# One core, conv-scan-attention block: a norm's factor moved behind its matmul, paired attention tiles, a split last projection, and new planner windows

## The chip, the cores and the metric

The kernel runs on one core of a Trainium2 chip. The metric is the device time of one execution in microseconds, taken as the median of several runs. Five engines work side by side, each on its own queue in order: PE (matmuls), DVE (VectorE), ACT (ScalarE), POOL (GpSimd) and SP, which here issues every DMA.

## What is computed

Input x is 8 images of 384 channels and 32 x 32 pixels, so 1024 tokens each. Two layers follow each other.

```
layer 0   xn  = rmsnorm over channels (x)
          per direction (forward, backward): u, z = in_proj(xn); u = silu(conv1d4(u))
              dt, B, C = x_proj(u);  delta = softplus(dt_proj(dt))
              h_t = exp(delta * A) * h_(t-1) + delta * u * B      384 channels x 16 states, 1024 steps
              y = sum over states(h * C) + u * D;   out_proj(y * silu(z))
          x1  = x + res * (scale * (fwd + bwd) + sigmoid(dwconv3x3(xn)) * xn)
layer 1   x2  = x1 + Wo * causal attention(layernorm(x1)), 6 heads of 64
          out = x2 + kron(p1, p2) * gelu(kron(f1, f2) * layernorm(x2))      (384 -> 1536 -> 384)
```

A layernorm subtracts the mean over the 384 channels and divides each token by its deviation. The first matmul of the last block is linear in the channels and has no bias, so a factor per token can be applied in front of it or behind it.

## The kernel before

The tiles are channels on the 128 partitions (three tiles of 128 channels) by 1024 tokens; HALF is 512 tokens, one PSUM bank of float32.

*The scan* (`scans` and `group`). For every image there are 96 steps: six blocks of 64 channels, two directions, and eight groups of 8 channels x 16 states = 128 rows. A step loads delta broadcast to the states into a tile dA (a DMA, 512 KB, of 12 such slots), takes its exp on ACT (L1007), spreads delta * u over the states with two matmuls into a ring of three PSUM banks, multiplies the two banks by B on DVE (L1035), scans 1024 tokens on DVE (L1041), multiplies by C on POOL (L1045) and sums the states on PE into the bank y. The operand of the spread is a tile du, loaded from DRAM array dusd, where delta * u lies as three bf16 parts (`delta`: POOL subtracts what was cast, L926, ACT casts the next part, L918, a DMA writes it).

*Around the scan*, for each image b: `project` (rmsnorm and in_proj of u), `gates` (in_proj of z), `prepare` (conv1d, x_proj), `deltas` (softplus and the parts), `local` (the 3 x 3 convolution), `finish` (out_proj, L1076 adds into x1), `layernorm`, `attention`, `mix` (Wo), `forward` (the last block).

*Attention* (`attend`): for each pair of heads and each 128 queries, the keys up to the diagonal come in one or two segments of up to 512. Scores on PE, maximum on DVE (L1201), exp on ACT (L1208), division on POOL (L1254), transposes of 128 x 128 on PE into a PSUM bank (L1261), copy to SBUF on ACT (L1268), context on PE. Weights p and their transposes pT had one tile for each head, 1024 keys wide.

*The norm* (`layernorm`): the mean comes from a matmul with ones (pm), DVE subtracts it (L1096), ACT squares (L1106), a matmul with ones sums (pv), ACT takes ln and exp in place for 1/deviation, and DVE multiplies each of the six half tiles by it (L1120). `forward` then multiplies by kr1 (py), copies to y (L1352), and goes on with the wide layer (ph, gelu, pz) and the last matmul (pe).

*The order.* Nothing runs in the order of the source. Each operation is recorded with an estimated cost and a due time; `Plan.run` then does a list scheduling over the five queues and four shared PSUM banks, 26 general SBUF slots and the slots of the scan, and the result is written out as a fixed order per engine. Due times come from windows: `stretch(span, b)` spreads a stage's operations over span x PERIOD after HEAD + b x PERIOD. The due time decides which of several ready operations goes first; on the chip nothing waits for it. The images overlap: while image b is scanned, b + 1 is prepared (`deltas`), b + 2 projected, and layer 1 of b - 1 runs. From image 2 to image 5 the order repeats.

Two lines set what follows from a window:

```
o.at = self.t0 + (self.t1 - self.t0) * done / total - early
a = o.at - (self.STAY if e == "ACT" and o.table in (None, table) else 0.0)
```

Of the kernel before, what the change touches and what calls it, by code (L numbers as in the profile page):

```python
# [12 lines left out]
ALU = mybir.AluOpType  # L13
# [4 lines left out]
P = 128  # L18
# [265 lines left out]
def conv_attn_hybrid_kernel(  # L284
# [49 lines left out]
    def half(hf):  # L334
        return slice(hf * HALF, (hf + 1) * HALF)

    def chans(c):
        return slice(c * P, (c + 1) * P)
# [94 lines left out]
    def bank(name):  # L433
        return Val("psm", [P, HALF], name)
# [12 lines left out]

    EVICT, MOVE, SUMS, PRODUCTS, DECAY, LOAD, PARTS = 154.0, 6.5, 31.9, 10.24, -27.73, -210.33, -103.58  # L450

    PROJECT, GATES, CONV, DELTA = (-1.488, -1.378), (-1.161, -1.106), (-0.901, -0.877), (-0.865, -0.39)
    LOCAL, OUTPUT, NORM, ATTEND = (0.78, 0.902), (0.999, 1.029), (1.126, 1.206), (1.226, 1.771)
    MIX, FORWARD = (1.75, 1.765), (1.898, 1.935)

    PROJECT0, EARLY, CONV0, DELTA0 = (-166.005, -75.933), (-268.945, -79.299), (87.042, 114.273), (95.896, 180.005)
    GATES0, LATE, PROJECT1, GATES1 = (198.993, 214.377), (111.423, 394.173), (-14.138, 120.69), (257.236, 258.236)
    CONV1, DELTA1, LAYER1 = (241.746, 250.867), (238.85, 495.647), (502.538, 846.683)

    class Window:  # L460

# [586 lines left out]
    def finish(b, x1):  # L1048

        s = b % 2  # L1050
        yg = []
        wo = tl(f"wout_{b}", [P, CT, C])
        dma(lambda: wo.t, lambda: out_wT.rearrange("(c p) e -> p c e", p=P), [], [wo], P * CT * C * 4)
        for c in range(CT):
            t = tl(f"yg_{b}_{c}")
            for a in range(2):
                v = ygd[s][2 * c + a]
                dma(
                    lambda t=t, a=a: t.t[a * HC : (a + 1) * HC, :], lambda v=v: v.t.rearrange("(h p) t -> p h t", p=HC),
                    [v], [(t, a)], HC * L * 4,  # L1060
                )
            yg.append(t)
        for m in range(CT):
            for hf in range(NH):
                p = bank(f"pg_{b}_{m}_{hf}")

                accumulate(
                    [
                        (lambda p=p, m=m, hf=hf, c=c: (p.t, wo.t[:, c, chans(m)], yg[c].t[:, half(hf)]), [yg[c], wo])
                        for c in range(CT)  # L1070
                    ], p, pe(HALF), [x1[m]],
                )

                def add(p=p, m=m, hf=hf):
                    t = x1[m].t[:, half(hf)]
                    nc.vector.scalar_tensor_tensor(t, p.t, rsm.t, t, ALU.mult, ALU.add)  # L1076

                op("DVE", dve(HALF), add, [p, rsm], [(x1[m], hf)])
            dma(lambda m=m: x1d[s].t[chans(m)], lambda m=m: x1[m].t, [x1[m]], [(x1d[s], m)], P * L * 4)

    def layernorm(dst, src, n):

        for hf in range(NH):
            p = bank(f"pm_{n}_{hf}")

            accumulate(
                [(lambda p=p, hf=hf, c=c: (p.t, ones, src[c].t[:, half(hf)]), [(src[c], hf)]) for c in range(CT)],  # L1090
                p, pe(HALF), dst,
            )
            for c in range(CT):
                op(
                    "DVE", dve(HALF),
                    lambda p=p, hf=hf, c=c: nc.vector.scalar_tensor_tensor(  # L1096
                        dst[c].t[:, half(hf)], p.t, -1.0 / C, src[c].t[:, half(hf)], ALU.mult, ALU.add
                    ), [p, (src[c], hf)], [(dst[c], hf)],
                )
        for hf in range(NH):  # L1100
            sqs = [tl(f"lsq_{n}_{hf}_{i}") for i in range(2)]
            p = bank(f"pv_{n}_{hf}")
            for c in range(CT):
                op(
                    "ACT", act(HALF),
                    lambda hf=hf, c=c, sqs=sqs: nc.scalar.activation(  # L1106
                        sqs[c // 2].t[:, half(c % 2)], dst[c].t[:, half(hf)], AF.Square
                    ), [(dst[c], hf)], [(sqs[c // 2], c % 2)], holds=sqs,
                )
            accumulate(  # L1110
                [
                    (lambda p=p, c=c, sqs=sqs: (p.t, ones, sqs[c // 2].t[:, half(c % 2)]), [(sqs[c // 2], c % 2)])
                    for c in range(CT)
                ], p, pe(HALF),
            )
            op("ACT", 2 * act(HALF) + 0.1, lambda p=p: rsqrt_mean(p.t, eps5), [], [p], table=EXP)
            for c in range(CT):
                op(
                    "DVE", dve(HALF),
                    lambda p=p, hf=hf, c=c: nc.vector.tensor_mul(dst[c].t[:, half(hf)], p.t, dst[c].t[:, half(hf)]),  # L1120
                    [p], [(dst[c], hf)],
                )

    def attention(b, x1):
# [45 lines left out]
        def attend(hp, i):  # L1170
# [3 lines left out]
            top, bottom = slice(0, HD), slice(HD, P)  # L1174
            nk = (i + 1) * P
            segs = [(k0, min(nk, k0 + HALF)) for k0 in range(0, nk, HALF)]
            ps = [tl(f"p_{n}_{hh}") for hh in range(2)]

            mx = Val("sm", [P, 2, 2], f"mx_{n}")
            den = Val("sm", [P, 2, 2], f"den_{n}")  # L1180
            for g, (k0, k1) in enumerate(segs):
# [23 lines left out]
                for hh in range(2):  # L1205

                    def exps(sc=sc, g=g, k0=k0, k1=k1, hh=hh):
                        nc.scalar.activation(  # L1208
                            ps[hh].t[:, k0:k1], sc[hh].t[:, 0 : k1 - k0], AF.Exp, bias=mx.t[:, g, hh : hh + 1],
                            accum_out=den.t[:, g, hh : hh + 1],  # L1210
                        )

                    op(
                        "ACT", act(k1 - k0) + 0.25, exps, [(mx, (g, hh)), sc[hh]], [(ps[hh], g), (den, (g, hh))],
                        table=EXP,
                    )
            if len(segs) > 1:
# [27 lines left out]
                op("POOL", 0.35, scales, [fac], [den])  # L1245
            else:
                op("DVE", 0.16, lambda: nc.vector.reciprocal(den.t[:, 0, :], den.t[:, 0, :]), [], [den])
            pT = [tl(f"pT_{n}_{hh}", [P, L // P, P]) for hh in range(2)]
            for g, (k0, k1) in enumerate(segs):
                for hh in range(2):  # L1250

                    def norm(g=g, hh=hh, k0=k0, k1=k1):
                        t = ps[hh].t[:, k0:k1]
                        nc.gpsimd.tensor_scalar(t, t, den.t[:, g, hh : hh + 1], 1.0, ALU.mult, ALU.mult)  # L1254

                    op("POOL", 0.15 + (k1 - k0) * 1.06e-3, norm, [den], [(ps[hh], g)])
                    t = bank(f"t_{n}_{g}_{hh}")

                    def turn(t=t, hh=hh, k0=k0, k1=k1):
                        for j in range(k0 // P, k1 // P):  # L1260
                            nc.tensor.transpose(  # L1261
                                t.t[:, j * P - k0 : (j + 1) * P - k0], ps[hh].t[:, j * P : (j + 1) * P], ident
                            )

                    op("PE", 0.05 + 0.12 * (k1 - k0) / P, turn, [(ps[hh], g)], [t], holds=pT)

                    def keep(t=t, hh=hh, k0=k0, k1=k1):
                        nc.scalar.copy(  # L1268
                            pT[hh].t[:, k0 // P : k1 // P, :].rearrange("p j t -> p (j t)"), t.t[:, 0 : k1 - k0]
                        )  # L1270

                    op("ACT", act(k1 - k0), keep, [t], [(pT[hh], g)])
            pc = bank(f"pc_{n}")

            cT = cTs[hp]
            for j0 in range(0, i + 1, 4):

                def context(js=range(j0, min(j0 + 4, i + 1))):
                    for j in js:
                        for hh, rows in enumerate((top, bottom)):  # L1280
                            mm(
                                pc.t[rows, 0:P], v.t[:, j * P + hh * HD : j * P + (hh + 1) * HD], pT[hh].t[:, j, :],
                                j == 0, j == i,
                            )

                op(
                    "PE", 0.05 + 0.24 * min(4, i + 1 - j0), context, [(t, j0 // 4) for t in pT] + [(v, j0 // 4)], [pc],
                    holds=[cT],
                )

# [44 lines left out]
    def forward(b, x2):  # L1335

        xn2 = [tl(f"xn2_{b}_{m}") for m in range(CT)]
        layernorm(xn2, x2, f"f{b}")
        y, z = tl(f"fy_{b}"), tl(f"fz_{b}")
        for hf in range(NH):  # L1340
            p = bank(f"py_{b}_{hf}")
# [8 lines left out]
                ], p, pe(HALF), [y],  # L1350
            )
            op("ACT", act(HALF), lambda p=p, hf=hf: nc.scalar.copy(y.t[:, half(hf)], p.t), [p], [(y, hf)])  # L1352
        for hf in range(NH):
            pz = bank(f"pz_{b}_{hf}")
            for a in range(FT // RG):
# [43 lines left out]

    PERIOD, HEAD = 417.04, 72.53

    def stretch(span, b):
        return Window(span[0] * PERIOD, span[1] * PERIOD, HEAD + b * PERIOD)
# [19 lines left out]
    for b in range(B):  # L1425
# [13 lines left out]
        with stretch(OUTPUT, b):  # L1439
            finish(b, x1)  # L1440
        with stretch(NORM, b):
            layernorm(x1, x1, f"a{b}")
        with stretch(ATTEND, b):
            cTs = attention(b, x1)
        with stretch(MIX, b):
# [79 lines left out]
```

## Time and profile before

| what | us |
|---|---|
| median of 3 runs | 4113.69 (4110.54 to 4115.77) |
| the profiled execution | 4114.34 |
| its span, first to last instruction | 4112.4 |
| first scan starts / last scan starts | 164.1 / 3837.8 |
| busy: PE, DVE, ACT, POOL | 3511.7, 3430.8, 2815.4, 3000.8 |
| mean granted clock of PE | 0.926 |
| DMA | 859 MB, mean 209 GB/s |

A row of the groups reads: line, engine, operation, output <- inputs, shapes, count, then busy microseconds and mean nanoseconds of one, then idle time of the engine just before these and what ended it. A row of the stretches gives the stretch, its length, and for each engine the busy time and the number of instructions, then the granted PE clock, the DMA share and GB/s. A row of the waits reads: who waited for whom, the total, how often, the longest. A row in order of time begins with start and duration; SPq is the DMA queue. Each float32 matmul of the program leaves two records.

### The profile page before, as it was taken

Reading aid. Unit: us, or ns where it says so; the run is one execution under the profiler, and the core shown is the slowest. Engines: PE = TensorE matmul, PEld = TensorE weight load, DVE = VectorE, ACT = ScalarE, POOL = GpSimd, SP = SyncE. Lnnn points to the kernel's source line nnn. Section 1 sums busy time; section 2 is a strip of 40 time slices with the busy share of each in tenths; the row PEclk is TensorE's granted clock in tenths of the full one; section 3 lists DMA queues with packets and bytes.
Section 4 is the critical chain, followed back from the end, with each engine's and each line's share of the span. In section 5 each row is a group of like instructions: output and inputs, shape, how many; then the busy total and the mean of one; then the engine's idle time right before and its main releaser. Section 6 shows DMA issues by size and latency. Waiting matters only on the chain. (4 is left out here: it accounts for less than half of the span.)

```text
span 4112.4 us, 54637 instructions
## 1 busy us (share of the span) xinstructions
PE 3511.7 (85%) x17970; PEld 1407.7 (34%) x17970; DVE 3430.8 (83%) x3661; ACT 2815.4 (68%) x4547; POOL 3000.8 (73%) x2370
## 2 busy tenths in 40 slices
PE   6466658899998999898998899988999888898898
PEld 2111112443234422443234432444234432443363
DVE  2399989989989899888989899889998899999522
ACT  3766447775787758885778857786787766665364
POOL 1889786997589955997579965998479965775231
PEclk9687679899999999899999999999998899999999
DMA  7899897579976898669976798669975697559100
GB/s 243 233 258 275 254 263 203 156 227 256 265 207 181 233 265 242 189 207 240 271 211 196 218 260 248 197 199 246 253 230 174 177 255 203 141 161 228 48 9 35
DMA packets 302003, 858.96 MB, mean 209 GB/s; under 512 B 38312, under 2 KB 91576, under 8 KB 301720
## 3 DMA queue, kind: packets, MB, share of 16 engines
q1 hardware_dynamic: 301720, 855.47, 74.6%
q8 instruction: 143, 2.34, 0.2%
q14 instruction: 140, 1.15, 0.1%
HBM read 696.44 MB, written 160.68 MB: 208 GB/s over the span
## 5 line engine op out<-in xcount | busy, mean ns | idle before, releaser
L1045 POOL TENSOR_TENSOR dA<-dA,bc 128x1024 f32<-128x1024 f32 x768 | 1810.6, 2365 | 724.5 <-DVE dA L1041 638.7
L1041 DVE TENSOR_TENSOR_SCAN dA<-dA,ring 128x1024 f32<-128x1024 f32 x768 | 1755.5, 2286 | 91.4 <-ACT dA L1007 27.6
L1035 DVE TENSOR_TENSOR ring<-ring,bc 128x512 f32<-128x512 f32 x1536 | 1071.2, 697 | 286.1 <-PE ring L327 171.8
L1007 ACT ACTIVATE dA<-dA,nA 128x1024 f32<-128x1024 f32 x768 | 860.8, 1145 | 249.8 <-DMA dA<-ded 245.1
L327 PE MATMUL ring<-du,dup 32*128 32x512 bf16 x1536 | 318.6, 410 | 384.4 <-DVE dA L1041 339.0
L327 PE MATMUL y<-dA,sel 128*32 128x512 f32 x3072 | 533.5, 659 | 28.6 <-POOL dA L1045 26.2
L1208 ACT ACTIVATE p<-s,mx 128x512 f32<-128x512 f32 (+3 forms) x576 | 330.9, 581 | 99.7 <-DVE mx L1201 98.8
L1201 DVE TENSOR_REDUCE mx<-s 128x1 f32<-128x512 f32 (+3 forms) x576 | 286.0, 546 | 134.1 <-PE s L327 130.4
L1254 POOL TENSOR_SCALAR p<-p,den 128x512 f32<-128x512 f32 (+3 forms) x576 | 329.1, 590 | 79.0 <-issue 47.0
L327 PEld LDWEIGHTS <-dup 32*128 32x128 bf16 x1536 | 73.1, 92 | 887.1 <-DVE dA L1041 779.9
L1268 ACT COPY pT<-t 128x512 f32<-128x512 f32 (+3 forms) x576 | 258.1, 483 | 163.1 <-PE t L1261 156.2
L1261 PE MATMUL t<-ident,p 128*128 128x128 f32 x1728 | 298.1, 304 | 74.3 <-ACT pT L1268 26.2
L327 PE MATMUL s<-k,q 64*128 64x512 f32 (+3 forms) x1152 | 301.8, 571 | 20.6 <-ACT p L1208 19.1
L327 PE MATMUL pi<-xp,win 128*128 128x512 f32 x576 | 287.7, 621 | 3.5 <-DMA win<-in_in_wT 2.0
L1261 PEld LDWEIGHTS t<-ident,p 128*128 128x128 f32 x1728 | 206.1, 152 | 212.1 <-POOL p L1254 83.7
L1461 ACT ACT_TABLE_LOAD x210 | 269.4, 1283 | 4.5 <-PEq L1514 0.8
L327 PE MATMUL pc<-pT,v 128*64 128x128 f32 x3456 | 261.9, 294 | 10.1 <-ACT pT L1268 5.6
L327 PEld LDWEIGHTS pc<-pT,v 128*64 128x64 f32 x3456 | 204.4, 146 | 105.6 <-ACT pT L1268 38.6
L918 ACT CAST part<-u 128x1024 bf16<-128x1024 f32 x144 | 150.3, 1044 | 88.7 <-POOL u L926 49.1
L926 POOL TENSOR_TENSOR u<-u,part 128x1024 f32<-128x1024 f32 x96 | 205.0, 2135 | 5.6 <-ACT part L918 5.5
L327 PEld LDWEIGHTS y<-dA,sel 128*32 128x32 f32 x3072 | 82.3, 113 | 287.2 <-issue 137.9
L327 PEld LDWEIGHTS s<-k,q 64*128 64x128 f32 x1152 | 116.7, 197 | 144.4 <-ACT p L1208 64.4
(183 smaller groups left out, 4714.5 us busy)
## 6 DMA issues: line engine op xcount, KB each, us to landing
dA<-ded SPq DMA_DIRECT2D x768, 512.0 KB
ct<-urd SPq DMA_DIRECT2D x96, 513.5 KB
du<-dusd SPq DMA_DIRECT2D x96, 512.0 KB
xs<-xpd SPq DMA_DIRECT2D x96, 432.8 KB
dusd<-part SPq DMA_DIRECT2D x288, 128.0 KB
ded<-de SPq DMA_DIRECT2D x48, 512.0 KB
uz<-uzd SPq DMA_DIRECT2D x48, 512.0 KB
bc<-bcd SPq DMA_DIRECT2D x32, 512.0 KB
```

The costliest lines, as they stand in the source:

```text
L327: return nc.tensor.matmul(out_, lhsT=lhsT, rhs=rhs, start=first, stop=last)
L926: "POOL", pool(L), lambda part=part: nc.gpsimd.tensor_sub(du.t, du.t, part.t), [part], [du]
L1007: "ACT", act(L) + 0.1, lambda: nc.scalar.activation(dA.t, dA.t, AF.Exp, scale=nA.t[:, g : g + 1]),
L1035: uses("DVE", nc.vector.tensor_mul(to, to, bc.t[:, 0, half(hf)]), [bank_of(v)])
L1041: i = nc.vector.tensor_tensor_scan(dA.t[:, rev], dA.t[:, rev], t[:, rev], 0.0, ALU.mult, ALU.add)
L1045: op("POOL", pool(L), lambda: nc.gpsimd.tensor_mul(dA.t, dA.t, bc.t[:, 1]), [(bc, 1)], [dA], at=at - PRODUCTS)
L1201: lambda sc=sc, g=g, w=k1 - k0, hh=hh: nc.vector.tensor_reduce(mx.t[:, g, hh : hh + 1], sc[hh].t[:, 0:w], AX.X, ALU.max, negate=True), [sc ...
L1208: nc.scalar.activation(ps[hh].t[:, k0:k1], sc[hh].t[:, 0 : k1 - k0], AF.Exp, bias=mx.t[:, g, hh : hh + 1], accum_out=den.t[:, g, hh : hh + 1],
L1254: nc.gpsimd.tensor_scalar(t, t, den.t[:, g, hh : hh + 1], 1.0, ALU.mult, ALU.mult)
L1261: nc.tensor.transpose(t.t[:, j * P - k0 : (j + 1) * P - k0], ps[hh].t[:, j * P : (j + 1) * P], ident)
L1268: nc.scalar.copy(pT[hh].t[:, k0 // P : k1 // P, :].rearrange("p j t -> p (j t)"), t.t[:, 0 : k1 - k0])
L1461: nc.scalar.preload_act_table_set(table)
```

## The change

Four things.

1. `layernorm` is taken apart into `center` and `deviation`. The norm in front of attention does as before. `forward` calls `center` alone, multiplies the centered tiles by kr1, copies to y, and multiplies y by the reciprocal deviation: two multiplications of half a tile in place of six.
2. Attention's p and pT have one tile for each segment, both heads side by side. Where a segment is at most 256 keys wide, both heads' transposes share one PSUM bank, and one copy moves both.
3. `finish` of the last image (b = 7) goes through its three channel tiles in two rounds: the first two into one set of banks and additions, the third into another. All writes of x1 follow at the end.
4. The planner's offsets and windows have other numbers; PERIOD goes from 417.04 to 380.0, HEAD from 72.53 to 55.16.

```diff
-    EVICT, MOVE, SUMS, PRODUCTS, DECAY, LOAD, PARTS = 154.0, 6.5, 31.9, 10.24, -27.73, -210.33, -103.58
-    PROJECT, GATES, CONV, DELTA = (-1.488, -1.378), (-1.161, -1.106), (-0.901, -0.877), (-0.865, -0.39)
-    LOCAL, OUTPUT, NORM, ATTEND = (0.78, 0.902), (0.999, 1.029), (1.126, 1.206), (1.226, 1.771)
-    MIX, FORWARD = (1.75, 1.765), (1.898, 1.935)
-    PROJECT0, EARLY, CONV0, DELTA0 = (-166.005, -75.933), (-268.945, -79.299), (87.042, 114.273), (95.896, 180.005)
-    GATES0, LATE, PROJECT1, GATES1 = (198.993, 214.377), (111.423, 394.173), (-14.138, 120.69), (257.236, 258.236)
-    CONV1, DELTA1, LAYER1 = (241.746, 250.867), (238.85, 495.647), (502.538, 846.683)
+    EVICT, MOVE, SUMS, PRODUCTS, DECAY, LOAD, PARTS = 378.57, 8.84, 29.05, -33.72, -280.37, -106.53, -33.21
+    PROJECT, GATES, CONV, DELTA = (-1.517, -1.372), (-1.059, -1.044), (-0.974, -0.902), (-0.89, -0.378)
+    LOCAL, OUTPUT, NORM, ATTEND = (0.747, 0.863), (0.984, 1.059), (1.078, 1.215), (1.202, 1.761)
+    MIX, FORWARD = (1.773, 1.91), (1.878, 2.051)
+    PROJECT0, EARLY, CONV0, DELTA0 = (-158.79, -45.82), (-401.082, 13.743), (18.036, 30.11), (141.195, 199.74)
+    GATES0, LATE, PROJECT1, GATES1 = (139.669, 207.977), (180.295, 417.068), (127.039, 159.251), (258.653, 404.451)
+    CONV1, DELTA1, LAYER1 = (196.627, 281.428), (237.122, 484.505), (473.374, 474.374)
...
-        for m in range(CT):
-            for hf in range(NH):
-                p = bank(f"pg_{b}_{m}_{hf}")
+        rounds = (range(CT),) if b + 1 < B else (range(CT - 1), range(CT - 1, CT))
+        for cs in rounds:
+            for m in range(CT):
+                for hf in range(NH):
+                    p = bank(f"pg_{b}_{m}_{hf}_{cs[0]}")
...
-    def layernorm(dst, src, n):
+    def center(dst, src, n):
...
+    def deviation(dst, n, hf):
+        sqs = [tl(f"lsq_{n}_{hf}_{i}") for i in range(2)]
+        p = bank(f"pv_{n}_{hf}")
...
+        op("ACT", 2 * act(HALF) + 0.1, lambda: rsqrt_mean(p.t, eps5), [], [p], table=EXP)
+        return p
+    def layernorm(t, n):
+        center(t, t, n)
+        for hf in range(NH):
+            p = deviation(t, n, hf)
...
-            ps = [tl(f"p_{n}_{hh}") for hh in range(2)]
+            ps = [tl(f"p_{n}_{g}", [P, 2, HALF]) for g in range(len(segs))]
...
-            pT = [tl(f"pT_{n}_{hh}", [P, L // P, P]) for hh in range(2)]
+            pT = [tl(f"pT_{n}_{g}", [P, 2, HALF]) for g in range(len(segs))]
...
+                for hs in ((0, 1),) if 2 * w <= HALF else ((0,), (1,)):
+                    t = bank(f"t_{n}_{g}_{hs[0]}")
+                    for hh in hs:
...
-                    op("ACT", act(k1 - k0), keep, [t], [(pT[hh], g)])
+                    op("ACT", act(len(hs) * w), keep, [t], [(pT[g], hh) for hh in hs])
...
-        layernorm(xn2, x2, f"f{b}")
+        center(xn2, x2, f"f{b}")
...
+            q = deviation(xn2, f"f{b}", hf)
+            op(
+                "DVE", dve(HALF), lambda q=q, hf=hf: nc.vector.tensor_mul(y.t[:, half(hf)], q.t, y.t[:, half(hf)]),
+                [q], [(y, hf)],
+            )
...
-    PERIOD, HEAD = 417.04, 72.53
+    PERIOD, HEAD = 380.0, 55.16
```

## The prediction

> **What bounds the kernel now.** I read the page's groups first, then busy time by stretch, then the waits of VectorE, then the start and the tail in order of time. The three groups of one scan step:
>
> ```profile
> L1045 POOL TENSOR_TENSOR dA<-dA,bc 128x1024 f32<-128x1024 f32 x768 | 1810.6, 2365 | 724.5 <-DVE dA L1041 638.7
> L1041 DVE TENSOR_TENSOR_SCAN dA<-dA,ring 128x1024 f32<-128x1024 f32 x768 | 1755.5, 2286 | 91.4 <-ACT dA L1007 27.6
> L1035 DVE TENSOR_TENSOR ring<-ring,bc 128x512 f32<-128x512 f32 x1536 | 1071.2, 697 | 286.1 <-PE ring L327 171.8
> ```
>
> A step costs VectorE 2.286 + 2 x 0.697 = 3.68 us; 768 steps are 2826 us. The first scan starts at 164 us, the last ends at 3840 us, and the page's span is 4112.4 us (the profiled execution itself took 4114.3, the median of the runs is 4113.7, so no correction is needed). Busy time by stretch: the head, images 0 and 1, the repeating image 4, the tail, then image 4 in four quarters of 24 steps.
>
> ```profile
> core 0: us, PE busy (x) PEld busy (x) DVE busy (x) ACT busy (x) POOL busy (x), PEclk, DMA share, GB/s
> 0.00:164.00 164.00, 85.83 (x261) 35.85 (x261) 22.01 (x75) 89.55 (x111) 64.99 (x66) 0.79 0.74 230
> 164.00:572.00 408.00, 273.70 (x1036) 66.03 (x1036) 368.54 (x314) 236.94 (x255) 353.10 (x173) 0.77 0.92 263
> 572.00:1025.00 453.00, 383.96 (x2010) 155.58 (x2011) 411.87 (x427) 301.80 (x505) 375.66 (x292) 0.90 0.77 215
> ...
> 1966.00:2432.00 466.00, 420.57 (x2245) 170.16 (x2244) 425.59 (x450) 355.48 (x573) 373.21 (x291) 0.97 0.82 229
> ...
> 3840.00:4113.00 273.00, 250.60 (x1316) 129.00 (x1314) 72.53 (x146) 127.15 (x334) 56.88 (x146) 0.96 0.09 32
> ```
>
> ```profile
> 1966.00:2077.00 111.00, 101.94 (x439) 29.03 (x441) 105.18 (x102) 89.20 (x103) 57.53 (x25) 1.00 0.99 280
> 2077.00:2190.00 113.00, 103.55 (x486) 44.39 (x478) 101.19 (x103) 90.69 (x134) 97.96 (x53) 0.94 0.66 190
> 2190.00:2316.00 126.00, 110.47 (x648) 52.69 (x646) 110.32 (x127) 105.18 (x202) 122.84 (x127) 0.95 0.68 199
> 2316.00:2432.00 116.00, 104.62 (x679) 44.04 (x679) 108.91 (x121) 70.41 (x137) 94.88 (x89) 1.00 0.95 249
> ```
>
> VectorE is busy 425.6 of 466 us; in the first and last quarter 94%. PE looks as busy (90%), but in image 0 it is busy 67% and VectorE still 90%, with steps 4.0 us apart: what is left idle there is the small gap between dependent VectorE operations. So between first and last scan an operation taken off VectorE is worth about its own time. The third quarter has another limit: POOL is busy 122.8 of 126. What VectorE waits for in image 4 adds up to 19.6 us:
>
> ```profile
> DVE mx L1201 <- PE s L327: 6.4, 5, 4.2
> DVE ring L1035 <- PE ring L327: 6.3, 7, 1.8
> DVE dA L1041 <- ACT dA L1007: 3.2, 2, 1.8
> ```
>
> The tail (273 us) has PE busy 92%, VectorE 27%: PE work bounds it. The head ends with the first ring matmul, whose du tile arrives late:
>
> ```profile
> 151.87 0.32 SPq L428 DMA_DIRECT2D du<-dusd  x1
> ...
> 161.90 0.61 PE L327 MATMUL ring<-du,dup 32*128 32x512 bf16 x3 [30.66 <-DMA du<-dusd]
> ...
> 137.93 1.03 ACT L918 CAST part<-u 128x1024 bf16<-128x1024 f32 x1
> ```
>
> **The deviation behind the first matmul.** It removes 6 multiplications of xn per image and adds 2 of y. The row:
>
> ```profile
> L1120 DVE TENSOR_TENSOR xn<-pv_f,xn 128x512 f32<-128x512 f32 x48 | 30.0, 682 | 5.9 <-ACT pv_f L332 5.9
> ```
>
> Seven images do this between the first and the last scan: 28 operations fewer. By the mean of one that is 28 x 0.682 = 19.1 us. [...] The row's busy time, which counts overlaps once, is 30.0 / 48 = 0.625[...] and I take it: 28 x 0.625 = 17.5 us. The two sums differ by under 4 us.
>
> **Last out_proj in two parts.** For image 7 alone 6 more additions at 0.734 (the rows of xr<-pg). In the new order 4 of the 12 stand before the last scan and 8 behind it, where it was 6 behind: +4 x 0.73 = 2.9 us on VectorE. The PE queue behind the last ring matmul holds 9 pg matmuls instead of 16. In the trace the 16 leave 32 records (two each), 14.2 us busy, 0.44 each; 12 of them ran while the last yg was written and read (8.1 us), so they are covered. The exposed piece is the 20 records at 3854, 8.85 us, of which 12 (5.3 us) remain: -3.5 us. At the very end the deviation now comes behind y: for the second half its two rsqrt steps (0.65 + 0.58) and the table load (1.28) no longer lie under py's 2.7 us of matmuls. That costs up to 2.5 and saves the 3 multiplications that stood before it; I take +1.5. Tail: -2 us.
>
> **Weights of both heads in one tile.** Of the 12 segments per head pair 4 are at most 256 wide, and their two copies become one:
>
> ```profile
> L1268 ACT COPY pT<-t 128x256 f32<-128x256 f32 x96 | 33.6, 383 | 8.8 <-PE t L1261 7.8
> L1268 ACT COPY pT<-t 128x128 f32<-128x128 f32 x96 | 23.4, 270 | 17.8 <-PE t L1261 16.8
> ```
>
> 48 x (2 x 0.270 - 0.383) + 48 x (2 x 0.383 - 0.587, the 512 row) = 16 us of ScalarE in all. [...] Either way nothing on the path: ScalarE is busy 355 of 466 us. If ScalarE were the bound in the third quarter (105 of 126 us) it would be at most 2 us per image. Matmuls and transposes keep their number; a merged copy waits for both heads' transposes, 2 x 0.17 us, before the context matmuls: nothing while PE has the scan's work beside it, in the tail under 1 us each way.
>
> **The new windows.** The planner writes another order for every queue; PERIOD itself makes nothing wait. I counted each queue in both built orders and priced each operation by its row.
>
> Head. POOL does 17 large operations before its first product, not 24. The third bf16 part of du could have been cast at 129.2 (POOL's subtraction ends then), but ScalarE's order put a softplus and three exps waiting for DMA before it: 137.93. Then SP's order puts the other direction's part writes, a de write and two loads before du, which is issued 13 us after the cast. In the new order the third cast stands before all exps, and between its writes and du there is one de write. Estimate: ScalarE's first softplus ends at about 110 as before (the earlier transposed loads may win 6 us, a matmul of image 1's z projection put before px, waiting for its weights, gives them back); POOL's four operations to u, 9.4, then subtraction, sum, subtraction and another step, 9.0: 128.5; cast 129.5; the de write waits for two more POOL steps, 4.7: 134; du at 135, landing 10 us later as before: first scan at 147 to 149 instead of 164: -15. Bounds: 0 if du queues behind the eight dA loads before it (4 MB, 16 us at 250 GB/s), -25 if the px path wins too.
>
> Between the scans the work is the same, placed elsewhere. By quarter in a repeating image (rows' durations), VectorE: 109, 105, 114, 112 before, 97, 109, 110, 121 after; POOL: 58, 117, 133, 74 before, 58, 130, 121, 73 after. POOL's overfull third quarter is evened, but second and third hold 250 and 251, so I give it 0; what it could bring is the idle of those quarters beyond the gaps, about 6 us per image. Image 1 takes over attention work: its VectorE sum goes from 423 to 432, image 6's from 443 to 433. That nets to nothing. VectorE's waits (19.6 us per image) I leave as they are: 0, with -6 to +15 per image as bounds, since any queue's order can help or hurt.
>
> **Sum** against the profiled 4114.3: head -15, VectorE -17.5 + 2.9, tail -2: -31.6, so about **4082 us**.
>
> **Rivals.** (1) *Evened POOL frees VectorE.* For: POOL 97% busy in the third quarter and the waits for exps there, which hang on dA tiles that POOL has not finished. Against: POOL's sum over both quarters is unchanged. 6 us in 5.5 images: 33 more, 4049. (2) *The head gains nothing*, as du waits behind the dA loads: 4097. (3) *Slower, through VectorE waiting in order.* The softmax maxima stand in VectorE's queue before scan steps, and wait for PE's scores; if the new order places them further ahead of what PE delivers, every scan behind stands too, and with it POOL's products and the dA tiles. In before this is 6.4 us for maxima and 6.3 for the ring in an image. It decides from 31.6 / 6 = 5.3 us more per image; at twice the present waits, +19 in six images, the time is 4082 + 114 = 4196; at 12 more, 4154. (4) *The change does nothing*: the removed multiplications fall into times when VectorE waited anyway, and the head is as before: 4112. Against it: 94% in the quarters where forward lies.
>
> **Chances.** Forecast 0.46 (its own range 4066 to 4096), rival 1 0.18, rival 2 0.14, rival 3 0.16, rival 4 0.06. A measurement of this kernel tells about 0.2% (8 us) from no change. Faster: 0.46 + 0.18 + 0.14 and nothing of the others: 0.78. Same: rival 4 and the first steps of rival 3: 0.08. Slower: 0.14. The range takes in the forecast, rival 2 and most of rival 1, and the near part of rival 3: 4038 to 4128.
>
> **What would show it.** Right: first scan near 148; 3635 VectorE records in place of 3661 and its busy sum down by about 16; the repeating image at 463 instead of 466 (2.5 us for its four multiplications); POOL's third quarter well under 97%; after the last scan one yg load, and 12 pg records behind it. Wrong: a repeating image over 470 with more waits of mx for s or of dA for exps; a first scan after 160; or a tail over 275.

## The result and the profile after

The changed kernel takes 4108.7 us (median of 20 runs, 4080.6 to 4125.4), the kernel before 4116.7 (20 runs, 4108.9 to 4141.0). The ratio is 0.9965 with a 95% interval of 0.995 to 0.998: about 14 us faster (8 to 21), where 32 were forecast. The ratio is not the quotient of the two medians, which lie 8 us apart; it agrees with the averages, 4105.5 and 4119.6. The first ten runs of the changed kernel average 4110.7 and the second ten 4100.3, so its own time is known to some 5 us only. The forecast had the direction and not the size.

The three groups of a scan step on the page of the changed kernel are as they were:

```profile
L1045 POOL TENSOR_TENSOR dA<-dA,bc 128x1024 f32<-128x1024 f32 x768 | 1808.7, 2365 | 736.9 <-DVE dA L1041 643.2
L1041 DVE TENSOR_TENSOR_SCAN dA<-dA,ring 128x1024 f32<-128x1024 f32 x768 | 1755.6, 2286 | 92.5 <-ACT dA L1007 26.3
L1035 DVE TENSOR_TENSOR ring<-ring,bc 128x512 f32<-128x512 f32 x1536 | 1071.0, 697 | 234.8 <-PE ring L327 125.1
```

Busy time by stretch, as in the prediction: the head, image 0, image 1, the repeating image 4, image 6, the tail, and then image 4 in quarters of 24 steps.

```profile
core 0: us, PE busy (x) PEld busy (x) DVE busy (x) ACT busy (x) POOL busy (x), PEclk, DMA share, GB/s
0.00:153.00 153.00, 97.16 (x287) 39.91 (x288) 21.73 (x75) 78.96 (x102) 46.15 (x58) 0.90 0.72 232
153.00:558.00 405.00, 248.11 (x957) 52.72 (x956) 368.69 (x313) 223.21 (x236) 339.77 (x167) 0.68 0.91 253
558.00:1030.00 472.00, 406.18 (x2139) 166.92 (x2137) 420.16 (x439) 332.39 (x534) 407.40 (x307) 0.93 0.82 228
1968.00:2433.00 465.00, 426.97 (x2249) 169.71 (x2245) 423.90 (x447) 352.27 (x560) 373.04 (x291) 0.98 0.82 228
2903.00:3392.00 489.00, 434.44 (x2222) 172.29 (x2220) 420.67 (x441) 355.98 (x559) 371.84 (x285) 0.93 0.78 212
3842.00:4111.00 269.00, 246.23 (x1299) 124.32 (x1298) 71.84 (x143) 125.55 (x321) 57.17 (x146) 0.94 0.10 33
1968.00:2073.00 105.00, 94.36 (x358) 26.72 (x354) 96.57 (x87) 76.99 (x87) 57.78 (x25) 0.97 0.90 247
2073.00:2190.00 117.00, 108.30 (x528) 44.59 (x524) 104.83 (x111) 95.54 (x144) 102.08 (x64) 0.97 0.72 205
2190.00:2309.00 119.00, 106.91 (x620) 50.27 (x620) 107.24 (x120) 99.25 (x185) 117.02 (x116) 0.97 0.68 198
2309.00:2433.00 124.00, 117.41 (x748) 48.14 (x747) 115.26 (x132) 80.49 (x146) 96.15 (x90) 1.00 0.97 263
```

The work came off VectorE as counted: 3635 records for 3661, 3418.2 us busy for 3430.8 (-12.6). The quarters of image 4 hold 97, 105, 107 and 115 us of it, where 97, 109, 110 and 121 were worked out (by the operations' own durations, which count overlaps twice). But the time did not follow. An image is counted here from its first scan to that of the next:

| stretch | before | after | difference | forecast |
|---|---|---|---|---|
| to the first scan | 164.1 | 153.5 | -10.6 | -15 |
| image 0 and image 7 | 863.6 | 854.3 | -9.2 | -4.6, images 1 and 6 included |
| images 2 to 5 | 1877.1 | 1872.3 | -4.8 | -10 |
| images 1 and 6 | 935.3 | 961.9 | +26.6 | new order: "nets to nothing" |
| behind the last scan | 272.3 | 268.2 | -4.1 | -2 |
| span | 4112.4 | 4110.2 | -2.2 | -31.6 |

The two profiled executions lie only 2 us apart and so show little of the 14 us. One execution scatters: images 2 and 3 of the changed kernel have one and the same order on VectorE, and their last quarters take 133.3 and 124.5 us. Part of such scatter goes with PE's granted clock. In five traces with the order of before (the kernel before and four of the experiments), the third quarters of images 2 to 5 took 128.4 to 130.5 us where the clock was 0.92 or less, and 126.2 to 127.6 where it was 0.95 or more; which of the two comes first is not shown. A single stretch is therefore read here to some 5 to 10 us, unless other images or runs repeat it.

The growth of images 1 and 6 is repeated. In the four experiments below that keep the order of before, image 1 took 453 to 455 us and image 6 468 to 476; in two that keep the new order they took 471 and 467, and 487 and 489.

Image 1 took over 8.3 us of VectorE work and, what the prediction did not count, 22.2 us of PE work (384.0 to 406.2 us, 129 more records). Its last quarter grew most, from 116.6 to 132.6 us: VectorE has 7.4 us more to do there, and its waits rose from 3.5 to 12.8 us, the largest of which is

```profile
DVE ring L1035 <- PE ring L327: 5.1, 3, 3.9
```

Image 6 *lost* 9 us of VectorE work and became longer. Before, it was

```profile
2902.00:3384.00 482.00, 430.82 (x2249) 176.68 (x2251) 429.62 (x457) 358.69 (x577) 371.80 (x286) 0.93 0.78 215
```

Its first and last quarters lost 9.5 and 7.7 us of VectorE work and became 4.0 shorter and 0.4 longer. Its second and third gained 3.7 and 5.1 us and became 5.2 and 5.9 longer. The third is also where POOL is fullest, at 132.3 of 136 us, where it had 123.4 of 130:

```profile
3129.00:3265.00 136.00, 120.99 (x783) 62.82 (x781) 113.38 (x141) 111.42 (x232) 132.29 (x135) 0.92 0.57 162
```

In this quarter VectorE stands before softmax maxima for 13.8 us, where it did so for 1.2 in the kernel before:

```profile
DVE mx L1215 <- PE s L327: 13.8, 6, 5.9
DVE ring L1035 <- PE ring L327: 3.1, 8, 0.5
```

```profile
DVE mx L1201 <- PE s L327: 1.2, 2, 0.9
```

That looks like the cause, but all waits of VectorE in the quarter sum to 18.3 us after and 17.1 before: the maxima took the place of other waits. The quarter's growth is the work moved into it, on VectorE and POOL; which of the two counts was not separated.

### The profile page after: what moved, and what is told of

The parts are those of the page before. It is cut to its first block, busy times and chain, and to the rows that moved or that the text cites. A ratio compares the mean times of both kernels' runs of the same rounds, so it can differ in the third digit from the quotient of the medians.

```text
span 4110.2 us, 54336 instructions
## 1 busy us (share of the span) xinstructions
PE 3542.8 (86%) x17970; PEld 1392.7 (34%) x17970; DVE 3418.2 (83%) x3635; ACT 2801.9 (68%) x4454; POOL 2998.9 (73%) x2370
## 4 chain that ended last, share of the span: by engine, by line
DVE 32%; POOL 21%; PE 21%; DMA 14%; issue 7%; ACT 5%; SPq 1%; DVEq 0%; POOLq 0%; ACTq 0%
DVE dA L1041 18%; DVE ring L1035 10%; POOL dA L1045 8%; DMA dA<-ded 5%; POOL p L1269 3%; DMA xs<-xpd 3%; PE y L327 2%; PE t L1279 2%; PE pc L327 2%; POOL w L911 2%; POOL de L912 2%; POOL de L913 2%; PE s L327 2%; PE ring L327 2%; PE pi L327 1%
## 5 line engine op out<-in xcount | busy, mean ns | idle before, releaser
L327 PE MATMUL y<-dA,sel 128*32 128x512 f32 x3072 | 544.1, 667 | 21.0 <-POOL dA L1045 12.4
L1215 DVE TENSOR_REDUCE mx<-s 128x1 f32<-128x512 f32 (+3 forms) x576 | 287.0, 546 | 128.1 <-PE s L327 118.8
L327 PE MATMUL s<-k,q 64*128 64x512 f32 (+3 forms) x1152 | 312.1, 552 | 22.2 <-ACT p L1222 20.0
L1286 ACT COPY pT<-t 128x512 f32<-128x512 f32 (+1 forms) x480 | 246.8, 548 | 116.7 <-PE t L1279 113.5
L1279 PE MATMUL t<-ident,p 128*128 128x128 f32 x1728 | 278.6, 297 | 48.9 <-POOL p L1269 32.3
L327 PE MATMUL pc<-pT,v 128*64 128x128 f32 x3456 | 247.7, 284 | 6.9 <-ACT pT L1286 6.3
L327 PEld LDWEIGHTS pc<-pT,v 128*64 128x64 f32 x3456 | 190.2, 139 | 98.2 <-ACT pT L1286 33.9
L327 PEld LDWEIGHTS s<-k,q 64*128 64x128 f32 x1152 | 118.0, 189 | 157.2 <-ACT p L1222 76.7
```

The lines of the kernel that those rows point to most:

```text
L327: return nc.tensor.matmul(out_, lhsT=lhsT, rhs=rhs, start=first, stop=last)
L1215: lambda sc=sc, g=g, w=k1 - k0, hh=hh: nc.vector.tensor_reduce(mx.t[:, g, hh : hh + 1], sc[hh].t[:, 0:w], AX.X, ALU.max, negate=True), [sc ...
L1279: nc.tensor.transpose(t.t[:, o + j * P : o + (j + 1) * P], ps[g].t[:, hh, j * P : (j + 1) * P], ident)
L1286: nc.scalar.copy(pT[g].t[:, hs[0] : hs[-1] + 1, 0:w], t.t[:, 0 : len(hs) * w].rearrange("p (h w) -> p h w", w=w))
```

## The experiments

There were two kinds. Some leave the order of every queue as it was and put single operations in or out. The others change a part of the kernel or the planner's numbers, and the planner then writes a new order. Each run was timed beside the kernel before. The changed kernel was not timed again beside them: where a run is set against it, its ratio 0.9965 (0.995 to 0.998) is taken, and a difference of 10 us or less from it is uncertain.

**Four multiplications per image left out, in the order of before.** As a count, this is what the norm's part takes off VectorE in each image, and nothing else.

```diff
+                    if dst is src or c == 0:
                         nc.vector.tensor_mul(dst[c].t[:, half(hf)], p.t, dst[c].t[:, half(hf)])
```

> The kernel before, its order on every queue unchanged, with 4 of the 6 multiplications by the reciprocal deviation in each image's last block left out (channel tiles 1 and 2 stay undivided, so the output is another). It is the removed VectorE work alone. If VectorE bounds the stretch between first and last scan, as predicted, 28 operations at 0.625 us are worth 17.5 us: ratio 0.9957. If another resource (DMA in the quarters where the busy share is 0.95 to 0.99, or POOL in the third quarter) sets the pace there, 0 to 5 us: ratio over 0.9988.

Measured 4120.8 against 4122.3: ratio 0.9992 (0.998 to 1.0005). So some 3 us, with an interval from -2 to 8, where 17.5 were summed. The first quarter of image 4 in this run:

```profile
1974.00:2085.00 111.00, 101.84 (x439) 28.94 (x441) 102.88 (x98) 89.71 (x103) 57.42 (x25) 1.00 1.00 279
```

It is still 111 us long, though 4 operations shorter on VectorE (98 records for 102, 102.9 us for 105.2). What VectorE waits for in it is new:

```profile
DVE ring L1035 <- PE ph L327: 2.2, 1, 2.2
```

The 2.5 us taken out came back as one wait: VectorE now reaches the ring before PE has got past the last block's matmuls (py and ph), which stand ahead of the ring matmuls in PE's queue. In the kernel before, VectorE and PE come to this point almost together: VectorE waits there 0.2 us. Elsewhere in the quarter PE's ring matmuls wait for VectorE's scans, in small pieces:

```profile
PE ring L327 <- DVE dA L1041: 7.0, 13, 0.9
```

**The same with PE relieved too.** Twelve matmuls per image out as well, four each of pm, pv and py.

```diff
-                mm(*args(), first, last)
+                if not lean:
+                    mm(*args(), first, last)
+                elif first:
+                    mm(*args(), True, True)
```

> As e1 (the order of before, 4 multiplications left out per image) and also 12 of the 18 matmuls of the last block's norm and first layer (pm, pv, py: only channel tile 0 is summed, so the output is another). That is 24 records at 0.44 us, 10.6 us of PE work less per image, 74 us in the seven images between the first and last scan, and 10 us in the tail. If PE, in whose queue the ring matmuls stand behind such work, is what holds the first quarter: at least 5 us per image with the multiplications, 35 and more, plus the tail: below 4075 (ratio under 0.989). If DMA holds it (busy 0.99): the tail's 10 and little else, 4105 to 4112 (ratio 0.996 to 0.999). If VectorE: as e1 plus the tail, ratio 0.997.

Measured 4104.2 against 4120.7: ratio 0.996 (0.9943 to 0.9977), 16 us. About 10 of these lie behind the last scan, where PE is the bound (262 us for 272). The first quarter of image 4 went from 110.8 to 109.2 us (images 2 to 5: 110.8 to 111.6 before, 110.3 to 111.0 with the multiplications alone left out, 109.0 to 109.5 here):

```profile
1956.00:2065.00 109.00, 93.30 (x414) 24.54 (x416) 102.52 (x98) 88.92 (x102) 57.41 (x25) 0.97 0.98 286
```

VectorE's wait for ph is down to 0.5 us. PE alone was not the holder: by the expectation that would have brought a ratio under 0.989, and 8.5 us less PE work in this quarter brought 1.6 us. The reading that fits both runs is that VectorE is first and PE close behind: 2.5 us off VectorE alone bring nothing here, with PE's work gone as well they bring 1.6. The twelve matmuls were never left out alone, so how the 1.6 us divide is not shown. The ratio also fits what had been expected if DMA holds the quarter; the next run speaks against that.

**Without the output stores of images 0 to 6**, beside the four multiplications:

```diff
-            dma(lambda m=m: ob[m], lambda m=m: x2[m].t, [x2[m]], [], P * L * 4)
+            ... nc.sync.dma_start(ob[m], x2[m].t) if b + 1 == B else None ...
```

> As e1, and the stores of the final output of images 0 to 6 are left out (so most of the output is not written): 1.57 MB less DMA per image, in the first quarter, 5.6 us at 280 GB/s, and 21 issues less on SP's queue. If DMA holds the first quarter: 3 to 5.6 us per image, 20 to 39 in all: 4082 to 4102 (ratio 0.990 to 0.995). If PE holds it: as e1 (ratio 0.998 to 1.0005).

Measured 4124.8: ratio 1.0012 (0.9999 to 1.0025), nothing gained. Without the stores the DMA rate of that quarter is 261 GB/s, in place of 279, which is 2 MB less, and the quarter stays at 110.8 us. So the DMA share of 1.00 in the row does not mark what held the quarter.

**Four additions of Wo left out, in both orders.** They stand in the last quarter. VectorE's waits for others in it, in image 4, sum to 2.2 us in before and 4.5 in after (the expectations have 2 and 2.6).

```diff
+                    if m == 0:
                         nc.vector.scalar_tensor_tensor(t, p.t, col("bo", m), t, ALU.add, ALU.add)
```

> The kernel before in its own order on every queue; of the six additions that bring the attention's output projection into the residual (x<-po), four per image are not issued, so the result lacks them. They stand in the last quarter of an image's scan, where VectorE's idle time is 2 us of 116. Seven images x 4 x 0.735 us = 20 us of VectorE work between the scans. Theory A (where VectorE is idle for 2 us or less of a quarter it sets the pace, so an operation taken out there pays): 12 to 20 us faster, ratio 0.995 to 0.997. Theory B (VectorE and PE hold each other through the three ring banks everywhere, so one engine's work alone pays next to nothing, as with the four multiplications left out): 0 to 6 us faster, ratio 0.9985 to 1, and the idle time of VectorE in that quarter grows by 2 to 3 us.

> The same four additions per image not issued in the changed kernel, in its own order; the result lacks them. There they stand in the last quarter of an image's scan too, which is now the fullest: 33.7 us of other work beside the scan's 88.2, and 2.6 us idle of 124.5. The changed kernel is at 0.9965. Theory A: another 12 to 20 us, ratio 0.9917 to 0.9937, the last quarter of a repeating image at 121.5 to 122.5. Theory B: 0 to 6 us, ratio 0.995 to 0.9965, the quarter stays at 124.

Measured for before: ratio 0.9987 (0.9972 to 1.0002), 5 us of the 20. For after: 0.9948 (0.993 to 0.9966), which is 7 us under the changed kernel's 0.9965; the intervals overlap. Theory B holds for the first, and the second lies nearer to it. The last quarters of images 2 to 5 do not show a gain: they average 117.9 us before and 118.0 here, 128.3 after and 127.4 here. The row of the last quarter in the first run, and VectorE's waits there:

```profile
2325.00:2443.00 118.00, 105.97 (x678) 46.57 (x677) 106.52 (x118) 70.33 (x137) 94.98 (x89) 0.96 0.93 246
```

```profile
DVE mx L1201 <- PE s L327: 3.2, 2, 3.0
DVE ring L1035 <- PE ring L327: 2.2, 3, 1.7
```

VectorE's 108.9 us became 106.5 and its waits grew from 2.2 to 6.7 us. Before, neither of these two was among the waits of this quarter. That VectorE waited for only 2% of the quarter did not mean that it alone set the pace; PE was just behind it.

**Four operations put back, in the order of after.**

```diff
                 nc.vector.tensor_mul(y.t[:, half(hf)], q.t, y.t[:, half(hf)])
+                for _ in range(2):
+                    nc.vector.tensor_scalar_mul(q.t, q.t, 1.0)
```

> The changed kernel with its order, and 4 VectorE operations per image put back: behind each multiplication of y, two multiplications of the PSUM tile by 1.0. VectorE theory: 17 us slower than the changed kernel, about 4126 (ratio to before 1.0007). Another bound: as the changed kernel, 4108 to 4112 (ratio 0.9965 to 0.998).

Measured 0.9989 (0.9974 to 1.0005) against the changed kernel's 0.9965: 10 us more, of 19.4 put in (28 x 0.694). The traces do not place them: the last quarters of images 2 to 5, with two of the four in them, average 128.3 us in the changed kernel and 128.1 here, the first quarters, with the other two, 104.4 and 105.8. So a fixed order answered to 17 to 20 us of VectorE work with 3, 5 and 7 us where it was taken out, and with 10 where it was put in. The 7 and the 10 are within what is uncertain; none of the four comes near the full time.

**Each xs load issued twice, in the order of after.**

```diff
+                    for _ in range(2):
+                        nc.sync.dma_start(t.t[:, 0 : PADDED - DX + 1], src)
```

> The changed kernel with its order, and every load of an xs tile (12 per image, 433 KB) issued twice: 5.2 MB more per image, 20 us of all 16 DMA engines at 263 GB/s, in the quarter where DMA is busy 0.96. DMA theory (transfers set the last and first quarter of a repeating image): 12 to 20 us per image, 100 to 160 us in all: 4210 to 4270. VectorE theory: the loads lie ahead of their use and cost nothing but SP's issue, 12 x 0.6 = 7 us per image beside other work: under 30 us, below 4140.

Measured 4468.1: ratio 1.0825, 45 us per image, where at most 20 were expected. The rate in the last quarter of image 3 fell from 264 to 219 GB/s, so it wasn't the bytes. SP's queue stood at these loads:

```profile
SPq L822 <- DMA xs<-xpd: 69.1, 12, 9.6
```

This is a side of the edit that the expectation overlooked. The second load of a pair writes the tile that the first one fills, so SP waits until the first has landed before it issues the second: in the trace of this quarter such waits last 4 to 10 us each. The run therefore says nothing of bandwidth. It shows what a stop of SP does to VectorE, two stages on, at the ring:

```profile
DVE ring L1036 <- PE ring L327: 31.3, 7, 12.4
```

PE waits at the local convolution's matmuls for its tile (24.1 us), the ring matmuls stand behind them, and VectorE behind those. So 69 us of waits on SP came out as 31 us of waits on VectorE.

**The new windows without the rest.**

```diff
-    PERIOD, HEAD = 417.04, 72.53
+    PERIOD, HEAD = 380.0, 55.16
...
+    MIX, FORWARD = (1.773, 1.91), (1.878, 2.051)
```

> The kernel before with the new planner numbers (windows, offsets, PERIOD, HEAD) alone: 6 multiplications, single tiles, one out_proj. Prediction's steps: head -15, no VectorE gain: about 4100 (ratio 0.996). If the new order is what took the gain back (images 1, 2 and 6 are longer in the changed kernel's trace), and the removed work is worth its 17.5 us, this is slower than before by some 10: 4125. If the removed work is worth nothing, it equals the changed kernel within 5 us.

Measured 4256.9: ratio 1.0315 (1.029 to 1.034), about 130 us slower. The first scan started at 155 us, as in the changed kernel: the head's gain belongs to the windows. The last quarters of images 2 to 5 took 138 to 146 us.

**The changed kernel with the old norm**, and **with the old attention tiles.**

```diff
-        center(xn2, x2, f"f{b}")
+        layernorm(xn2, x2, f"f{b}")
```

> The changed kernel with the old norm in its last block (six multiplications in front of the matmul), everything else of the change and its planner numbers kept; the planner orders anew. If the removed multiplications are the gain: 4120 to 4126. If they are worth nothing by themselves (e1: 3 us) and the order decides: anything, and an increase over 20 us would say that the numbers fit only this set of operations, as with the windows alone (+132).

```diff
-            ps = [tl(f"p_{n}_{g}", [P, 2, HALF]) for g in range(len(segs))]
+            ps = [tl(f"p_{n}_{hh}") for hh in range(2)]
```

> The changed kernel with attention's old tiles and copies (one tile per head), all else kept. By the prediction the pairing is worth nothing: 4108 to 4115. If it is what lets the new windows fit (a block of up to 4 key tiles needs 2 of the 26 shared slots and not 4, so loads start earlier), most of the 132 us of the windows alone comes back: over 4200.

Measured 1.0062 (1.0043 to 1.008), 40 us above the changed kernel, for the norm, and 1.0206 (1.0189 to 1.0223), 99 us above it, for the tiles: over 4200, as was expected if the slots are the reason. By the steps of the prediction the first should have been 17.5 and the second nothing.

**The last out_proj in one round**, in the changed kernel, and **the new norm alone** in the kernel before.

```diff
-        rounds = (range(CT),) if b + 1 < B else (range(CT - 1), range(CT - 1, CT))
```

> The changed kernel with the last out_proj in one round, as before; all else as changed. By the prediction's steps the split cost 2.9 us on VectorE and brought 3.5 us of PE behind the last scan: about 1 us, ratio 0.9965 to 0.997, and the stretch behind the last scan 271 to 273 us in place of 268. If the split had been what shortened that stretch and more besides: ratio above 0.998.

> The kernel before with the deviation divided by behind the first matmul, all else old: old tiles, old windows, one round. The planner writes its order anew with fewer operations. By the prediction's step 17.5 us come off VectorE between the scans: ratio 0.9958. By the run that left the same multiplications out in the old order, 3 us: 0.999. If an order written anew for windows that were not made for it costs more than it brings, as with the new windows alone (+132) or the old tiles in the new windows (+98): 1.002 or more.

Measured 1.0018 (1.0003 to 1.0032), 22 us above the changed kernel; its stretch behind the last scan took 286 us, not 271 to 273, as the new order left more matmuls for it (1334 records for 1299). And 1.0103 (1.0079 to 1.0126), 42 us slower than before. So the new norm, the part that takes the work away, made the kernel *slower* when the planner wrote an order for it under the old windows.

These numbers are far beyond what the parts' operations cost. Either each part is worth that much, or a newly written order costs it. So the last two runs keep every operation.

**The changed kernel with a slightly smaller PERIOD.**

```diff
-    PERIOD, HEAD = 380.0, 55.16
+    PERIOD, HEAD = 379.5, 55.16
```

> The changed kernel, every operation kept, only PERIOD 379.5 in place of 380.0: the planner writes another order, in which large parts of all five queues differ. Theory A (the order as a whole decides, and taking parts back cost +22 to +98 us because each time another, unfitted order was written): slower than the changed kernel (0.9965) by 10 us or more, ratio 0.999 to 1.01. Theory B (the parts taken back were themselves worth those times): within 8 us of the changed kernel, ratio 0.9945 to 0.9985.

> As the last one with PERIOD 379.8: a third order from the same operations. Theory A: again 10 us or more slower than the changed kernel, but by another amount than with 379.5, ratio 0.999 to 1.01. Theory B: ratio 0.9945 to 0.9985.

Measured 1.0048 (1.0028 to 1.0068) and 1.0049 (1.0034 to 1.0065). Changing PERIOD by 0.05% or 0.13%, and no operation, costs 34 us: more than twice the whole gain of the change. Their intervals do not meet the changed kernel's. Theory A holds. (The same was not tried on the kernel before, so how its own order compares with its neighbours is not known.) In the first of them, the repeating image 4 has the work of the changed kernel (423.2 us on VectorE for 423.9) and takes 9 us longer:

```profile
1978.00:2452.00 474.00, 430.74 (x2246) 175.04 (x2246) 423.24 (x447) 357.38 (x564) 373.52 (x292) 0.95 0.82 225
```

VectorE's first two waits there are these:

```profile
DVE dA L1041 <- ACT dA L1007: 14.4, 6, 4.9
DVE ring L1035 <- PE ring L327: 13.6, 15, 2.7
```

In the changed kernel the same two are:

```profile
DVE ring L1035 <- PE ring L327: 6.1, 10, 1.2
DVE dA L1041 <- ACT dA L1007: 3.3, 3, 2.4
```

So the +22 of the unsplit kernel and the +40 of the old norm are about what a new order costs by itself, and say little of these parts. The +99 of the old tiles and the +130 of the windows alone go beyond it. Both have the old tiles under the new windows. An old tile is 1024 keys wide for each head, whatever the block of queries; a new one holds both heads' segment of up to 512 keys, so that a block with one segment takes one of the 26 shared slots for p and one for pT, not two each. With the old tiles the last quarter of image 4 takes 140.6 us, and VectorE waits in it 11.0 us for the ring and 5.3 for pw. That the slots are the cause is argued from the code, and the expectation had the size right; no run varied them alone.

## Why the prediction was right in direction and wrong in size

*What bounds the kernel now: the step that failed.* "So between first and last scan an operation taken off VectorE is worth about its own time." In the unchanged order it was worth about a fifth: 3 us of 17.5 for these very multiplications, 5 of 20 for another set. At the first figure, this one term is 14 of the 17 us by which the forecast missed. The argument leaned on VectorE's 94% and on image 0, where PE is 67% busy. The gaps of image 0 are there, 0.10 and 0.14 us in a step between 299 and 312 us. But image 0 has no layer 1 beside it. In the first quarter of image 4 PE was 92% busy at a clock of 1.00, and its own queue row had said so: its ring matmuls wait for VectorE in thirteen pieces, 0.9 us at most. VectorE and PE hand three ring banks back and forth, each in its own order; when VectorE got 2.5 us faster, PE was close behind and 2.2 us came back as a wait for it. The rows with DMA shares of 0.99 and 0.95 were shown and not used; this did no harm, as the run without stores showed.

*The deviation behind the first matmul: -17.5.* The count was right (28 operations fewer). The price was nearly so: VectorE's total fell by 12.6 us where "about 16" was to be seen, as each multiplication of y costs 0.68 us and not 0.625. The worth was not. Whether 0.625 or 0.68 us is taken for one does not matter beside that.

*The new windows, head: -15, measured -10.6.* The mechanism was right to the point where the queue is SP's. POOL finished u at 119.2 us (119.4 worked out) and the third cast began at 129.9 (it was to be done at 129.5). But du was issued at 147.8, not 135:

```profile
129.92 1.07 ACT L918 CAST part<-u 128x1024 bf16<-128x1024 f32 x1
134.19 6.16 SPq L428 DMA_DIRECT2D dusd<-part  x4
140.46 1.93 SPq L428 DMA_DIRECT2D ded<-de  x1
147.78 0.33 SPq L428 DMA_DIRECT2D du<-dusd  x1
151.25 0.61 PE L327 MATMUL ring<-du,dup 32*128 32x512 bf16 x3 [17.23 <-DMA du<-dusd]
```

The working had counted one de write between the part writes and du. It left out what SP waits for itself: between 131 and 149 us its queue waited 6.7 us for dA loads and 5.3 for the part writes. Against that du landed in 3.5 us, not 10. The term was mis-sized by 4 us, and it would have been by more without the second error.

*The new windows, between the scans: 0.* "That nets to nothing" failed, by +27 us for images 1 and 6 in the profiled pair, and by 11 to 22 us for each of them in other runs of the two orders. The sum counted VectorE only and let what leaves image 6 pay for what enters image 1. The traces show that work moved in counted, with PE's 22 us in image 1 not in the sum at all, and that work moved out paid little. Why the planner put it there was not settled. By the trace of image 4 POOL's second and third quarter went from 98.0 and 122.8 us to 102.1 and 117.0, less evened than the 117 and 133 to 130 and 121 that were counted by place in the queue.

*Weights of both heads in one tile: nothing.* As operations this was right: ScalarE's total fell by 13.5 us (2815.4 to 2801.9) and it was no bound. What was missed is what the tiles do to the order that the planner writes: with the old ones the new windows cost 99 us. In the tail they were put at "under 1 us each way"; see the next step.

*Last out_proj in two parts, tail: -2, measured -4.1.* That the sum came near is luck: up to the end of these matmuls the tail gained 1.2 us and not 3.5, and behind them it gained 2.9 where 1.5 were to be lost. The counts were right, 12 records behind the last yg and 8 additions, but their 5.3 us took 8.4:

```profile
3855.32 8.40 PE L327 MATMUL pg<-yg,wout 128*128 128x512 f32 x12 [3.51 <-DMA yg<-ygd]
```

The 12 pg records that had filled PE's wait for yg (5.3 us of it) were gone, PE stood still for 3.5 us, and the granted clock fell:

```profile
3855.30:3859.00 3.70, 3.68 (x5) 1.63 (x6) 0.75 (x1) 0.00 (x0) 0.00 (x0) 0.50 0.07 24
3859.00:3863.70 4.70, 4.70 (x10) 1.97 (x9) 3.00 (x4) 0.00 (x0) 0.00 (x0) 0.75 0.29 119
```

In the kernel before, PE's one gap between 3848 and 3863 us is 0.88 us, and the clock there was 1.00. Behind the gap of 3.5 us it was 0.50 for 3.7 us and 0.75 over the next 4.7, by estimate some 6 us at 0.50, if the rest was at 1.00. That the gap brought the fall is read from these two traces and was not tested alone; in the unsplit run the clock was 0.50 behind a gap of 2.1 us. On this reading the covered work that the prediction called free had a use.

From the end of these matmuls to the end of the span it is 246.5 us, where it was 249.4. The other traces tell more of these 3 us. Counted from the first matmul behind, it is 246.6 us in the changed kernel, 246.5 with the old norm in it and 249.6 with the old tiles in it: under the new windows the 3 us go with the tiles. But the new norm alone, under the old windows, has 246.6 too, so the norm can shorten this stretch as well. Each is one execution.

*Rivals.* The second (the head gains nothing) fell: -10.6. The first (evened POOL) saw the third quarter of image 4 fall from 126 to 119 us, with POOL still at 98% (117.0 of 119), but the second and fourth grew by 4 and 8 us, and it brought nothing. The third (maxima ahead of the scores) named the right danger, an order in which VectorE waits, but not the right place: the maxima's waits grew only where others went. The fourth had the reason that was largely true, "the removed multiplications fall into times when VectorE waited anyway", except that the waits came only once the work was gone. It had been given 0.06 because of the 94%.

## What to carry to other kernels

A busy share of 94% tells which engine is first, not how close the next one is: before an operation removed from it is given its own time, ask of the same stretch what the engine's partners in a shared ring wait for, and price the step by the distance to the second. Where a planner writes a fixed order, a change of the operations and the new order are two changes. Write the new order several times without changing any operation (here a PERIOD moved by 0.05% cost 34 us) before a difference is put down to the operations.

## What the runs showed of the hardware that was not expected

- After PE stood idle for 3.5 us its granted clock was 0.50, and 12 matmul records took 8.4 us in place of 5.3. In the unsplit run the clock was 0.50 already from 3858 to 3862 us, with gaps of PE of 2.10 us before 3856.0 and 2.08 us before 3860.0; it was 0.50 through a gap of 7.7 us too, and in the first 5.4 us of work behind it.
- The third quarter of an image took 128.4 to 130.5 us where the granted clock was 0.92 or less and 126.2 to 127.6 at 0.95 or more, with the same order and the same work: part of what looks like noise between executions is to be seen in the clock.
- A DMA share of 1.00 at 279 GB/s in a quarter was not what held it: with the stores taken out it ran at 261 GB/s, and the quarter was as long as before.
- Issuing one kind of load twice into the same tile cost 45 us per image while the rate fell to 219 GB/s, because SP waited for the first copy to land, 69 us in one quarter; ACT waited 15.5 us there for dA loads, which SP issues too.
